# A graph layer with gathered neighbour rows: 74 instead of 64 rows fetched one by one, in three parts per block

## The chip, the cores and the metric

The kernel runs on one core of a Trainium2 chip. The metric is the device time of one execution in microseconds (us). Four runs of the kernel before gave 15966.83 to 15967.91 us, with a median of 15967.28 us. The profile is that of one execution, which took 15966.83 us; its span, from the first to the last instruction that the profile shows, is 15964.8 us.

## The reference: what is computed

There are N = 50,000 nodes with D = 128 features in float32, and E = 1,650,000 edges, sorted by destination (every node also has an edge to itself). Cut to what matters:

```python
Xs = X[src]                                   # one row of 128 floats per edge
m_data = Xs @ W_data.T + b_data
m_ctrl = Xs @ W_control.T + b_control
msg = jnp.where((edge_types == 0)[:, None], m_data, m_ctrl)
agg = jax.ops.segment_sum(msg, dst, num_segments=X.shape[0])
out = relu(agg + (X @ W_self.T + b_self))
x = _layernorm(x + out, axis=-1)
```

The kernel sums the raw rows of each node by edge type first and multiplies by the weights afterwards, so that its main work is to fetch one row of 512 bytes per edge and to add it to the right node.

## The kernel before, in words

The edges are cut into blocks. Block 0 and the last one ("plain" blocks) hold gathered edges alone; each of the 509 blocks between them holds 3,234 edges in Q = 2 steps, and a step has three kinds of edges:

- 12 chunks of 126 edges. POOL fetches a chunk with one indirect DMA (`gathers`, L473), so a block has 24 of them, in four passes of six. TensorE multiplies the rows by a one-hot matrix into `acc` (L492).
- F = 41 "fillers". An edge whose source is its own destination needs no gathered row, for the node's row is in `xT` anyway. `fill` (L306 to L336, VectorE) puts the 41 fillers into the slots of such edges, and `left_out_*` put the left-out rows back. The program branches at L934 to a slow general form (`general`) if some step holds fewer than F such edges.
- S = 64 single rows, one DMA of 512 bytes each, from a register address. They are issued by the queues of SP and ACT, 32 each per step. `offsets` (L433, VectorE) writes the 128 byte offsets of a block into the tile `at_x`, two blocks ahead and one more. `single_rows` (L435) loads 32 of them into registers of the engine with one TENSOR_LOAD (L442) and issues 32 row DMAs into the tile `yx` (L447), a register move and a DMA_DIRECT2D each. `yx` has four slots. TensorE waits for all of a block's single rows at L456 before their product L498.

The order of instructions on each engine is the order of the program text (`manual_schedule`). In the main loop (L607 to L655) the list of SP for block b is: load of `xT` for block b + 3 (L403, with the five block bases loaded into registers by L397 every fifth block, and seven loads of edge lists every tenth block); offsets and 32 rows of step 0 of block b + 2 (after pass 0); the store of the finished rows of block b - 1 (L556, after pass 2), which waits for VectorE's `o` (L555); offsets and 32 rows of step 1. The list of ACT is: offsets and 32 rows of step 0; the square root for block b - 1 (`root`, L547), which waits for VectorE's `mv`; offsets and 32 rows of step 1. VectorE's `store` (L553) waits for that square root, and after it VectorE makes `fill` for block b + 5, `offsets` for b + 3 and the sums of the next block.

The first offset load of a block waits for VectorE's `at_x`, and its first row DMA for TensorE's last use of the `yx` slot. POOL waits only for a free slot of its `y` tiles (10 slots of one pass each) and for its indices.

The four tiles `at_x` start at multiples of 16 bytes within their partition, as the built program places them (byte 177,856 and further in steps of 512), and so does `base_i` (byte 40,000), from which L397 loads the five bases of blocks b to b + 4, at byte 40,000 + 4b.

Of the kernel before, what the change touches and what calls it, by code (L numbers as in the profile page):

```python
# [2 lines left out]

# [10 lines left out]
U8 = mybir.dt.uint8  # L14
# [10 lines left out]
ROW = 4 * D  # L25
# [10 lines left out]
Q = 2  # L36
PASS = 6
B = 112
C = R * Q
F = 41  # L40
S = 64
X = Q * S
R1 = R + 1
C1 = Q * R1
SIZES = [126] * R
SIZE = sum(SIZES)
CE = Q * SIZE
BE = CE + Q * F + X
NBLK = 2 + (E - CE) // BE
# [7 lines left out]
AHEAD = 2  # L57
# [17 lines left out]
TBL = GROUPS * GB  # L75
# [3 lines left out]
def plain(b):  # L79

    return b == 0 or b >= NBLK - 1
# [6 lines left out]
def straight(ctx, tc, c, x, x_t, src_t, dst_t, etype_t, src_f, dst_f, etype_f, src_x, dst_first, first_p, out):  # L88
# [13 lines left out]
    nc = tc.nc  # L102
# [21 lines left out]
                   allow_small_or_imprecise_dtypes=True)  # L124
    FILL = Q * F + C1
    small = keep_ps.tile([P, 2 * W + F + 2 * FILL + 2], F32, name="small")
    num_ps, rank_no_ps = small[:, :2 * W], small[:, 2 * W:2 * W + F]
    lists = [small[:, 2 * W + F + i * FILL:][:, :FILL] for i in range(2)]
    sums_at = [small[:Q * F, 2 * W + F + 2 * FILL + i:][:, :1] for i in range(2)]

# [80 lines left out]
    def clear_sums():  # L211
        for t in sums:
            nc.vector.memset(t, 0.0)
            nc.vector.memset(t[0:3, 2, :], 1.0)
            nc.vector.memset(t[0:2, 2, :], 0.0)
# [80 lines left out]
    def spread_out(g):  # L296
        vd_g[g] = dram.tile([GS * F], F32, name="vd")
        nc.sync.dma_start(vd_g[g].rearrange("(s f) -> s f", f=F), vp_g.pop(g))

    def spread_in(g):  # L300

        v = eds.tile([P, GB, Q, F], F32, name="vf_all")
        nc.sync.dma_start(v.rearrange("p b q f -> p (b q f)"), row_bcast(vd_g.pop(g)))
        v_g[g] = v
# [33 lines left out]
    def left_out_columns(b):  # L338

        if not plain(b):  # L340
            pc = sums_at[b % 2]
            nc.tensor.matmul(pc, bys.pop(b).rearrange("p q f -> p (q f)"), ones_b[:, 0:1], start=True, stop=True)  # L342
            pcs[b] = pc

    def left_out_matrix(b):
        if not plain(b):
            z = fil.tile([Q * F, 2, P], BF16, name="z", bufs=RAHEAD + 1)
            at = fil.tile([Q * F, 1], F32, name="at")
            nc.vector.tensor_copy(at, pcs.pop(b))
            nc.vector.tensor_scalar(z.rearrange("p t n -> p (t n)"), node_no, at, None, op0=ALU.is_equal)  # L350
            zs[b] = z
# [25 lines left out]
    def steps_of(b):  # L377
        return [q for q in range(Q) if len(chunks_of(b, q))]
# [8 lines left out]

    idxs = {0: idx0}
    bys, pcs, zs, pls, bases, ats, ys = {}, {}, {}, {}, {}, {}, {}
    ohs, cnts, accs, xTs, pos, hs, mvs, sds = {}, {}, {}, {}, {}, {}, {}, {}  # L390

    BASES = 5

    def window(b):
        if b % BASES == 0:
            n = min(BASES, NBLK - b)
            _, regs = nc.values_load_multi_w_load_instructions(  # L397
                base_i[0:1, b:b + n], engines=[SP], min_val=0, max_val=N - B,
                skip_runtime_bounds_check_because="it was clamped to this")
            bases.update({b + i: at for i, at in enumerate(regs)})  # L400
        at = bases[b]
        xT = stp.tile([P, B], F32, name="xT", bufs=5)
        nc.sync.dma_start(xT, x_t[:, bass.ds(at, B)])  # L403
        xTs[b] = xT

    def onehot(b):
        g, i = divmod(b, GB)
        oh = ohp.tile([P, C1, 2 * W], F32, name="oh")
        nc.vector.tensor_tensor(oh, col_g[g][:, i, :, None].to_broadcast([P, C1, 2 * W]),  # L409
                                num_ps[:, None, :].to_broadcast([P, C1, 2 * W]), op=ALU.is_equal)  # L410
        ohs[b] = oh

    def counts(b):

        cnt = ohp.tile([P, Q, 2 * W], BF16, name="cnt")
        with nc.allow_low_precision(reason="whole numbers up to R1"):
            nc.vector.tensor_reduce(cnt, ohs[b].rearrange("p (q r) w -> p q w r", r=R1), AX.X, ALU.add)  # L417
        cnts[b] = cnt
# [1 line left out]


    ROW_SLOTS = AHEAD + 2
    TURN = S // 2
    RANGE = dict(min_val=0, max_val=(N - 1) * ROW, skip_runtime_bounds_check_because="where a node's row is")
    x_bytes = x.rearrange("n d -> (n d)").bitcast(U8)[None, :]
    fetched = [[tc.alloc_semaphore(f"fetched{j}_{i}") for i in range(ROW_SLOTS)] for j in range(2)]
# [5 lines left out]
            ats[b] = stp.tile([1, X], I32, name="at_x", bufs=AHEAD + 2)  # L432
            nc.vector.tensor_scalar(ats[b], one_g[g][:, i * X:(i + 1) * X], float(ROW), None, op0=ALU.mult)  # L433

    def single_rows(b, q):  # L435

        if q == 0:
            ys[b] = stp.tile([S, Q, D], F32, name="yx", bufs=ROW_SLOTS)
        both = []
        for j, (eng, dma) in enumerate(((SP, nc.sync), (ACT, nc.scalar))):  # L440
            at = j * TURN
            _, rows = nc.values_load_multi_w_load_instructions(  # L442
                ats[b][0:1, q * S + at:q * S + at + TURN], engines=[eng], **RANGE)
            both.append([(dma, fetched[j][b % ROW_SLOTS], at + k, row) for k, row in enumerate(rows)])
        for pair in zip(*both):
            for dma, sem, k, row in pair:
                copy = dma.dma_start(ys[b][k:k + 1, q, :].bitcast(U8), x_bytes[:, bass.ds(row, ROW)])  # L447
                copy.then_inc(sem, 16)
                tc.no_tile_sem_insts.add(copy.ins.name)
                tc.add_to_no_dep_group(f"single{b}", copy.ins)  # L450

    def rows_fetched(b):

        times = len(range(b % ROW_SLOTS or ROW_SLOTS, b + 1, ROW_SLOTS))
        for j in range(2):
            wait = nc.tensor.wait_ge(fetched[j][b % ROW_SLOTS], 16 * Q * TURN * times)  # L456
        tc.declare_fence(wait.ins, group=f"single{b}")


# [24 lines left out]
    def products(b, q, ks):  # L484
# [9 lines left out]
        if ks[-1] == of_step[-1]:  # L494
            if not plain(b):
                if q == 0:
                    rows_fetched(b)
                nc.tensor.matmul(acc[:, :2, :].rearrange("p t w -> p (t w)"), ys[b][:, q, :],  # L498
                                 ohs[b][:S, q * R1 + R, :], start=False, stop=True)
            for t in range(2):  # L500
# [49 lines left out]
    def store(b):  # L550
        mv = mvs.pop(b)
        rstd = stp.tile([B, 1], F32, name="rstd")
        nc.vector.reciprocal(rstd, sds.pop(b))  # L553
        o = stp.tile([B, D], F32, name="o")
        nc.vector.tensor_scalar(o, hs.pop(b), mv[:, 0:1], rstd, op0=ALU.subtract, op1=ALU.mult)  # L555
        nc.sync.dma_start(out[bass.ds(bases.pop(b), B), :], o)  # L556

    def find_bad():

# [36 lines left out]
    for b in range(1, RAHEAD):  # L596
        fill(b)
        left_out_columns(b)
        left_out_matrix(b)
        if b < AHEAD:  # L600
            onehot(b)
            counts(b)
            for q in range(Q):
                single_rows(b, q)
        if b == 1:
            clear_sums()
    for b in range(NBLK + 1):  # L607
        if b == NBLK - 1:
            find_bad()
        if b + 3 < NBLK:  # L610
            window(b + 3)
        g, i = divmod(b, GB)
        if i == 0 and g + 1 < GROUPS:
            load_edges(g + 1)
        if i == 3 and g + 1 < GROUPS:
            spread_out(g + 1)
        if i == 4 and g + 1 < GROUPS:
            spread_in(g + 1)
        if b > 0:
            add(b - 1, steps_of(b - 1)[-1])  # L620
        if b < NBLK:
            begin_sums(b)
        last = steps_of(b)[-1:]
        for q, (step, ks) in enumerate(passes_of(b)):
            if ks:
                products(b, step, ks)
            if q == 0 and b > 0:
                layer(b - 1)
            if q == 1:
                left_out_numbers(b + 1)  # L630
            if q == 3:
                left_out_columns(b + RAHEAD)
            if ks and step not in last and ks[-1] == chunks_of(b, step)[-1]:
                add(b, step)
            if q == 0 and b > 0:
                moments(b - 1)
            if q == 0 and b + AHEAD < NBLK:
                onehot(b + AHEAD)
            if q == 1 and b > 0:
                root(b - 1)  # L640
            if q == 2 and b > 0:
                store(b - 1)
            if q == 1 and b + AHEAD < NBLK:
                counts(b + AHEAD)
            if q == 2 and i == 2 and g + 1 < GROUPS:
                columns(g + 1)
            if q == 2:
                left_out_rows(b + 1)
                if b + RAHEAD < NBLK:
                    fill(b + RAHEAD)  # L650
            if q == 3:
                left_out_matrix(b + RAHEAD)
                offsets(b + AHEAD + 1)
            if q % 2 == 0 and not plain(b + AHEAD):
                single_rows(b + AHEAD, q // 2)  # L655


def general(ctx, tc, c, x, src, dst, etype, out):
# [331 lines left out]
```

## Time and profile before

| what | value |
|---|---|
| median of four runs | 15967.28 us |
| the profiled execution / its span | 15966.83 us / 15964.8 us |
| POOL busy | 12208.2 us (76%), 12,247 gathers (12,240 and 7) |
| VectorE (DVE) busy | 10893.8 us (68%) |
| TensorE (PE) busy | 8286.1 us (52%), granted clock 0.54 |
| ACT busy | 153.8 us (1%) |
| row DMAs by the queue of ACT / of SP | 32,576 / 32,576, 0.5 KB each |
| mean share of the 16 DMA engines | about 0.2 |

The profile lists an engine's busy time for its computing instructions only. Register loads, register moves and the issue of a DMA are done by the engine's own instruction queue (ACTq, SPq in the views) and are not counted as busy, so the 1% of ACT says nothing about how full its queue is. In the groups of instructions, a row gives the line, engine and operation, the count, the busy time, the mean of one, and the idle time ahead of them with its releaser. The view of one source line gives, for each engine, least, median and largest duration in ns and the first and last start.

### The profile page before, as it was taken

The numbers are of one execution on the slowest core, as the hardware profiler recorded it, in microseconds if no ns is written. First come the engines' busy times: TensorE is split into PE (matmuls) and PEld (weight loads), VectorE is DVE, ScalarE is ACT, GpSimd is POOL, SyncE is SP. The second block draws the span as 40 slices with busy tenths as digits, with TensorE's granted clock in tenths as the row PEclk, the third lists the DMA queues.
The fourth block names the chain that finished last, engine by engine and source line by source line (L and its number), as shares of the span: only waits on it lengthen the run. The fifth ranks groups of instructions, "written<-read, shape, count | busy, mean of one in ns | idle before, by whom it ended". The sixth has DMA issues, their size and how long they took to land.

```text
span 15964.8 us, 246443 instructions
## 1 busy us (share of the span) xinstructions
PE 8286.1 (52%) x35890; PEld 7100.4 (44%) x35891; DVE 10893.8 (68%) x14042; ACT 153.8 (1%) x517; POOL 12208.2 (76%) x12257
## 2 busy tenths in 40 slices
PE   3555555555555555555555555555555555555555
PEld 3444444444444444444444444444444444444444
DVE  8766666666666667666766666666666667666765
ACT  0000000000000000000000000000000000000000
POOL 7777777777777777777777777777777777777777
PEclk7555555555555555555555555555555555555555
DMA  2222222222222222222222222222222222222222
GB/s 62 60 59 60 59 60 59 60 60 59 59 60 59 59 60 59 60 59 60 59 59 59 59 60 58 60 60 59 59 60 59 59 60 58 60 59 60 59 59 56
DMA packets 895864, 944.21 MB, mean 59 GB/s; under 512 B 401739, under 2 KB 715928, under 8 KB 894220
## 3 DMA queue, kind: packets, MB, share of 16 engines
q0 software_dynamic: 587872, 791.74, 18.5%
q1 hardware_dynamic: 240758, 119.60, 2.9%
q10 hardware_dynamic: 65590, 17.01, 0.5%
q14 instruction: 1352, 11.08, 0.2%
q8 instruction: 292, 4.78, 0.1%
HBM read 896.86 MB, written 29.47 MB: 58 GB/s over the span
## 4 chain that ended last, share of the span: by engine, by line
POOL 59%; issue 19%; PE 10%; DMA 6%; DVE 4%; PEld 0%; ACTq 0%; POOLq 0%; PEldq 0%; ACT 0%; SPq 0%; DVEq 0%
POOL y L473 59%; PE acc L492 6%; DMA y<-in_x,idx 6%; PE po L531 2%; PE po L529 1%; DVE cnt L417 1%; PE po L528 1%; DVE h L537 0%; DVE h L538 0%; DVE st L540 0%; PE po L527 0%; DVE by L335 0%; ACTq L447 0%; PEld acc L492 0%; DVE m L316 0%
## 5 line engine op out<-in xcount | busy, mean ns | idle before, releaser
L473 POOL DMA_INDIRECT y<-in_x,idx x12240 | 12199.7, 997 | 3736.0 <-issue 3619.7
L492 PE MATMUL acc<-oh,y 126*128 126x120 f32 x24494 | 5873.8, 429 | 7031.1 <-PEq L480 7001.9
L492 PEld LDWEIGHTS acc<-oh,y 126*128 126x128 f32 x24494 | 5310.2, 326 | 7464.8 <-PEq L480 7424.6
L417 DVE TENSOR_REDUCE cnt<-oh 128x240 bf16<-128x3120 f32 x511 | 2959.0, 5791 | 0.1
L537 DVE COPY h<-po 112x128 f32<-112x128 f32 x511 | 149.0, 292 | 3334.9 <-PE po L531 3323.0
L409 DVE TENSOR_TENSOR oh<-col,small 128x3120 f32<-128x3120 f32 x511 | 1722.9, 3372 | 0.0
L508 DVE TENSOR_TENSOR sums<-acc,sums 128x180 f32 x1021 | 352.6, 345 | 1143.8 <-PE acc L501 1098.6
L335 DVE TENSOR_REDUCE by<-old 128x82 bf16<-128x1066 f32 x509 | 1073.5, 2109 | 17.6
L498 PE MATMUL acc<-oh,yx 64*128 64x120 f32 x2036 | 782.5, 486 | 0.0
L316 DVE TENSOR_TENSOR m<-rk,small 128x1066 f32<-128x1066 f32 x509 | 644.4, 1266 | 17.4
L319 DVE TENSOR_TENSOR new<-m,small 128x1066 f32<-128x1066 f32 x509 | 644.4, 1266 | 17.3
L323 DVE TENSOR_REDUCE v_new<-new 128x26 f32<-128x1066 f32 x509 | 642.9, 1263 | 17.3
L332 DVE TENSOR_TENSOR old<-m,small 128x1066 f32<-128x1066 f32 x509 | 640.2, 1258 | 0.0
L498 PEld LDWEIGHTS acc<-oh,yx 64*128 64x128 f32 x2036 | 500.4, 305 | 211.4 <-issue 207.3
L531 PE MATMUL po<-wmsgT,sums 128*112 128x128 f32 x2044 | 527.3, 403 | 0.0
L531 PEld LDWEIGHTS po<-wmsgT,sums 128*112 128x112 f32 x2044 | 383.1, 258 | 111.3 <-issue 94.7
L342 PE MATMUL small<-ones_b,by 128*82 128x1 bf16 x509 | 113.0, 222 | 609.6 <-DVE by L335 605.1
L342 PEld LDWEIGHTS <-by 128*82 128x82 bf16 x509 | 75.6, 149 | 659.5 <-DVE by L335 655.7
L529 PE MATMUL po<-bias,sums 3*112 3x128 f32 x1022 | 356.6, 445 | 1.5 <-DVE sums L508 1.5
L528 PE MATMUL po<-wselfT,xT 128*112 128x128 f32 x1022 | 317.6, 413 | 0.0
L521 DVE TENSOR_TENSOR sums<-pl,sums 128x336 f32<-128x336 f32 x509 | 258.3, 507 | 85.5 <-DVE sums L508 84.9
L547 ACT ACTIVATE sd<-mv,eps 112x1 f32<-112x1 f32 x511 | 150.6, 295 | 15690.9 <-DVE oh L409 7651.5
(119 smaller groups left out, 4201.9 us busy)
## 6 DMA issues: line engine op xcount, KB each, us to landing
yx<-in_x ACTq DMA_DIRECT2D x32576, 0.5 KB
yx<-in_x SPq DMA_DIRECT2D x32576, 0.5 KB
y<-in_x,idx POOLq DMA_INDIRECT x12240
xT<-in_x_t SPq DMA_DIRECT2D x511, 56.0 KB
out<-o SPq DMA_DIRECT2D x511, 56.0 KB
vf_all<-vd SPq DMA_DIRECT2D x52, 410.0 KB
s<-in_src_t SPq DMA_DIRECT2D x52, 130.0 KB
d<-in_dst_t SPq DMA_DIRECT2D x52, 130.0 KB
```

Of the source, the lines that this page charges most:

```text
L316: nc.vector.tensor_tensor(m, rk_g[g][:, i, :, None].to_broadcast([P, C1, F]), rank_no_ps[:, None, :].to_broadcast([P, C1, F]), op=ALU.is_e ...
L319: nc.vector.tensor_tensor(new.rearrange("p (q r) f -> p q r f", r=R1), m.rearrange("p (q r) f -> p q r f", r=R1), vf.rearrange("p (q f) -> ...
L323: nc.vector.tensor_reduce(v, new, AX.X, ALU.add)
L332: nc.vector.tensor_tensor(old, m, cb[:, :, None].to_broadcast([P, C1, F]), op=ALU.mult)
L335: nc.vector.tensor_reduce(by, old.rearrange("p (q r) f -> p q f r", r=R1), AX.X, ALU.add)
L409: nc.vector.tensor_tensor(oh, col_g[g][:, i, :, None].to_broadcast([P, C1, 2 * W]), num_ps[:, None, :].to_broadcast([P, C1, 2 * W]), op=AL ...
L417: nc.vector.tensor_reduce(cnt, ohs[b].rearrange("p (q r) w -> p q w r", r=R1), AX.X, ALU.add)
L473: copy = nc.gpsimd.indirect_dma_start(out=y[:r, k % PASS, :].bitcast(U8), out_offset=None, in_=x_rows, in_offset=bass.IndirectOffsetOnAxis ...
L492: nc.tensor.matmul(acc[:, :2, :].rearrange("p t w -> p (t w)"), y[:r, k % PASS, :], ohs[b][:r, column(k), :], start=k == of_step[0], stop= ...
L498: nc.tensor.matmul(acc[:, :2, :].rearrange("p t w -> p (t w)"), ys[b][:, q, :], ohs[b][:S, q * R1 + R, :], start=False, stop=True)
L529: nc.tensor.matmul(po, a[0:3, 2, :B], bias, start=False, stop=False)
L531: nc.tensor.matmul(po, a[:, t, :B], c["wmsgT"][:, t * D:(t + 1) * D], start=False, stop=t == 1)
```

## The change

S becomes 74: of each step's single rows SP fetches 36 and ACT 38. F becomes 42. A block then holds 3,256 edges, there are 505 full blocks instead of 509 (507 with the plain ones, instead of 511), and the last block holds 2,696 edges in 22 chunks instead of 870 in 7.

A block's single rows are no longer loaded by step but by engine: in the list of offsets stand first the 72 of SP, then the 76 of ACT, and each engine takes its own in three parts (24, 24 and 24 for SP; 25, 25 and 26 for ACT), after passes 0, 1 and 2. ACT's offsets start at elements 72, 97 and 122 of `at_x`. The tile has 148 elements of 4 bytes, and its slots again start at multiples of 16 bytes. The store of the finished rows stands after pass 3 now, behind all of SP's rows. The order of the other work is the same. In the changed file L442, L447, L547, L553 and L556 are L446, L451, L551, L557 and L563.

```diff
-F = 41
-S = 64
+F = 42
+TURNS = (36, 38)
+S = sum(TURNS)
+LOADS = 3
...
-    def single_rows(b, q):
-
-        if q == 0:
+    def single_rows(b, part):
+
+        if part == 0:
             ys[b] = stp.tile([S, Q, D], F32, name="yx", bufs=ROW_SLOTS)
         both = []
         for j, (eng, dma) in enumerate(((SP, nc.sync), (ACT, nc.scalar))):
-            at = j * TURN
-            _, rows = nc.values_load_multi_w_load_instructions(
-                ats[b][0:1, q * S + at:q * S + at + TURN], engines=[eng], **RANGE)
-            both.append([(dma, fetched[j][b % ROW_SLOTS], at + k, row) for k, row in enumerate(rows)])
-        for pair in zip(*both):
-            for dma, sem, k, row in pair:
-                copy = dma.dma_start(ys[b][k:k + 1, q, :].bitcast(U8), x_bytes[:, bass.ds(row, ROW)])
+            n = Q * TURNS[j]
+            k0, k1 = part * n // LOADS, (part + 1) * n // LOADS
+            at = Q * sum(TURNS[:j])
+            _, rows = nc.values_load_multi_w_load_instructions(ats[b][0:1, at + k0:at + k1], engines=[eng], **RANGE)
+            both.append([(dma, fetched[j][b % ROW_SLOTS], *divmod(k0 + k, TURNS[j]), sum(TURNS[:j]), row)
+                         for k, row in enumerate(rows)])
+        for pair in zip_longest(*both):
+            for dma, sem, q, k, at, row in filter(None, pair):
+                copy = dma.dma_start(ys[b][at + k:at + k + 1, q, :].bitcast(U8), x_bytes[:, bass.ds(row, ROW)])
                 copy.then_inc(sem, 16)
...
-            wait = nc.tensor.wait_ge(fetched[j][b % ROW_SLOTS], 16 * Q * TURN * times)
+            wait = nc.tensor.wait_ge(fetched[j][b % ROW_SLOTS], 16 * Q * TURNS[j] * times)
...
-        nc.sync.dma_start(out[bass.ds(bases.pop(b), B), :], o)
+        os_[b] = o
+
+    def store_rows(b):
+        nc.sync.dma_start(out[bass.ds(bases.pop(b), B), :], os_.pop(b))
...
-            for q in range(Q):
-                single_rows(b, q)
+            for part in range(LOADS):
+                single_rows(b, part)
...
-            if q % 2 == 0 and not plain(b + AHEAD):
-                single_rows(b + AHEAD, q // 2)
+            if q < LOADS and not plain(b + AHEAD):
+                single_rows(b + AHEAD, q)
+            if q == LOADS and b > 0:
+                store_rows(b - 1)
...
-        ones[1:] = steps[:, :, SIZE + F:].reshape(TBL - 1, X)
+        single = steps[:, :, SIZE + F:]
+        ones[1:] = np.concatenate([single[:, :, sum(TURNS[:j]):][:, :, :n].reshape(TBL - 1, Q * n)
+                                   for j, n in enumerate(TURNS)], axis=1)
```

More of the change, by code (lines that the diff above doesn't have):

```diff
@@ L2 @@
 from contextlib import ExitStack
+from itertools import zip_longest
 import concourse.bacc as bacc
@@ L389, in straight @@
     bys, pcs, zs, pls, bases, ats, ys = {}, {}, {}, {}, {}, {}, {}
-    ohs, cnts, accs, xTs, pos, hs, mvs, sds = {}, {}, {}, {}, {}, {}, {}, {}
+    ohs, cnts, accs, xTs, pos, hs, mvs, sds, os_ = {}, {}, {}, {}, {}, {}, {}, {}, {}
     BASES = 5
@@ L422, in straight @@
     ROW_SLOTS = AHEAD + 2
-    TURN = S // 2
     RANGE = dict(min_val=0, max_val=(N - 1) * ROW, skip_runtime_bounds_check_because="where a node's row is")
```

## The prediction

> **What bounds the kernel now.** I read the chain that ended last first, then the two costliest groups.
>
> ```profile
> POOL 59%; issue 19%; PE 10%; DMA 6%; DVE 4%; PEld 0%; ACTq 0%; POOLq 0%; PEldq 0%; ACT 0%; SPq 0%; DVEq 0%
> ...
> L473 POOL DMA_INDIRECT y<-in_x,idx x12240 | 12199.7, 997 | 3736.0 <-issue 3619.7
> L492 PE MATMUL acc<-oh,y 126*128 126x120 f32 x24494 | 5873.8, 429 | 7031.1 <-PEq L480 7001.9
> ```
>
> POOL's gathers lead the chain. One takes 997 ns, and the idle time ahead of them is nearly all "issue": POOL waits for nobody, it needs 0.30 us between two gathers. The view of line L473 has the first gather at 3.2 us and the first of the last seven at 15938.1: 15,934.9 us for 12,240, **1.302 us each, 31.25 us per block of 24**. The PE row says the reverse: PE waits for rows. So POOL is saturated, and any engine that needs under 31.25 us per block is free.
>
> Next come the queues, which the busy shares leave out. The timeline of one block (from the start of a line's first row DMA; rows of one line are merged), for ACT and then for SP:
>
> ```profile
> 8013.16 10.67 ACTq L447 DMA_DIRECT2D yx<-in_x  x32
> 8023.93 0.30 ACT L547 ACTIVATE sd<-mv,eps 112x1 f32<-112x1 f32 x1 [28.90 <-DVE oh L409]
> ```
>
> ```profile
> 8014.04 0.36 SPq L403 DMA_DIRECT2D xT<-in_x_t  x1
> 8016.62 10.66 SPq L447 DMA_DIRECT2D yx<-in_x  x32
> 8032.94 0.34 SPq L556 DMA_DIRECT2D out<-o  x1
> ```
>
> 32 rows take some 10.7 us, and 2 us pass ahead of them. That is the load of their offsets, in the view of line L442, whose three durations are least, median and largest in ns:
>
> ```profile
> L442 ACTq TENSOR_LOAD <-at_x x1018: 2112/2145/2417, 16.9 to 15862.6; - x170
> L442 SPq TENSOR_LOAD <-at_x x1018: 1864/2066/2272, 26.9 to 15872.9; - x170
> ```
>
> All those loads start at a multiple of 16 bytes. The changed ones don't, so I looked for loads that don't now. L397 loads five bases at byte 40,000 + 4b. Here are those for b = 20, 25, 30 and 35, and the last, of a single one, for b = 510; modulo 16 their bytes are 0, 4, 8, 12 and 8.
>
> ```profile
> L397 SPq TENSOR_LOAD <-base_i x1: 789/789/789, 555.7 to 555.7; - x1
> L397 SPq TENSOR_LOAD <-base_i x1: 1342/1342/1342, 706.0 to 706.0; - x1
> L397 SPq TENSOR_LOAD <-base_i x1: 1345/1345/1345, 860.5 to 860.5; - x1
> L397 SPq TENSOR_LOAD <-base_i x1: 1330/1330/1330, 1016.9 to 1016.9; - x1
> L397 SPq TENSOR_LOAD <-base_i x1: 537/537/537, 15854.6 to 15854.6; - x1
> ```
>
> **This decides my forecast.** In the whole trace each of the 26 loads of five at a multiple of 16 takes 0.75 to 0.96 us, and each of the 76 others 1.33 to 1.55, with the same registers in turn; so it is the address. Misaligned, one register takes 0.54 and five 1.34: **0.20 us per further register**. Aligned, five take 0.79 and 32 take 2.07: 1.28 us for 27 more, **0.19 us per further group of four** (0.047 per register). I read it as accesses of 0.2 us, which bring four registers from an aligned start and one otherwise. At offset 12, one register and then an aligned four would be two accesses, as at offset 0, but the row shows 1.33 and not 0.79: the load doesn't fall back into fours on its way.
>
> A page of the Trainium skill speaks against every load here: "Runtime: NRT & Kernel Launch", section "Instruction fetch mechanics", puts register loads at about 200 ns per register, even in bulk. The 2.07 us for 32 contradict it for aligned loads (it would give 6.4), and 0.20 per further register agrees for misaligned ones. By the rule for all three loads (76 x 0.2 = 15.2 us) ACT would need 41.2 us per block and the kernel some 20,900 us, an estimate.
>
> **The change part by part.**
>
> *Fewer gathers.* Edges: (1,650,000 - 3,024) / 3,256 gives 505 full blocks and 2,696 edges over. Gathers: 24 x 506 + 22 = 12,166, against 12,247. 81 x 1.302 = 105.5 us less on POOL, all on the path as long as POOL sets it.
>
> *ACT's list.* Three loads. The first starts at byte 288 of its tile (a multiple of 16): 25 registers, 2.145 - 7 x 0.047 = 1.81 us. The second starts at byte 388, the third at 488: 4 and 8 modulo 16. 25 misaligned registers: 1.34 + 20 x 0.20 = 5.34, and ACT's loads take 1.04 times SP's (2.145 / 2.066): 5.55 us. 26: 5.76 us. Together 13.1 us, against 4.3 now.
> Rows: within a part, from the third row on, ACT issues one per 0.3245 us (mean in the trace; median 0.318), and 0.41 us per part lies around its load and first row (a part of 32 takes 12.95 us in the mean: 2.15 + 32 x 0.3245 + 0.41). 76 rows: 24.7 + 3 x 0.41 + 0.1 for the square root's start = 26.0 us. **ACT needs 26.0 + 13.1 = 39.1 us per block**, against 25.9 now (with over 5 us of waiting), and POOL 31.25. Nothing hides the difference: ACT becomes the bound.
>
> *SP's list.* 72 rows at 0.3275 us = 23.6; 0.16 around each of three loads = 0.5; three loads of 24 (bytes 0, 96, 192, all aligned): 3 x (2.066 - 8 x 0.047) = 5.1; the store 0.55 and `xT` 0.6 with what lies around them; the bases 0.25, edge lists and spreads 0.4 in the mean. 31.0 us: just below POOL and well below ACT. The store now stands behind all rows. At its old place SP waited for `o` (1601.0 us in the waits of SP's queue), with 32 rows queued behind it. `o` comes 22 us after the block's `at_x`, and SP's rows now take about 29: the wait goes, and what it held up, `xT` for three blocks ahead, is not needed for long. Price nothing, between -0.1 and +0.3 us per block.
>
> *VectorE and PE.* 42 instead of 41 fillers lengthen five operations of 7.2 us together (L316, L319, L323, L332, L335) by 2.4%: 0.17 us. VectorE is busy 21.3 of 31.25 us, so this is hidden; without cover it is 88 us. PE's single-row product has 74 rows for 64 and the same 120 columns; the rows of L492 (126) and L498 (64) show no growth with rows. Nothing.
>
> *Where the wait shows.* The square root stands between ACT's first and second part, and VectorE's `store` waits for it, with fill, the next `at_x` and the sums queued behind it. From there to the next `mv` VectorE needs 20 us, and to the next `at_x` 10 us; ACT brings 39 and 28 us of its own work in that time. So ACT never waits: VectorE waits for ACT, PE for VectorE, and POOL for slots.
>
> **Sum.** The first square root starts at 116.7 us; ACT then has 503 blocks of rows: 503 x 39.1 = 19,667. About 60 us follow the last row (two blocks' products, sums and stores; now it is 89 us, with gathers at POOL's pace in it). Span 19,840 or, with a third of a block already issued at 116.7, 19,828, and 2.0 us around the span as now: **19,830 us, 24% more than before**. The profiled execution lies 0.45 us below the median, so no correction.
> Bounds: with rows at the median 0.318, no factor 1.04 and 0.18 per register (five misaligned against five aligned are three accesses more for 0.55 us), the loads take 12.0 us and ACT 37.5: 19,030. With 0.24 per register (ACT's 2.145 against 0.463 for its single load of `bad`, L934, are seven accesses more) and 0.33 per row, the loads take 14.4 us and ACT 40.8: 20,690.
>
> **The rivals.**
>
> *No fee for misalignment in long loads* (the other side). Against it: 76 of 76 rows of five. For it: no misaligned load of more than five is in the trace. Loads of 1.81, 1.81 and 1.86 make ACT 31.5 us, a hair over POOL. The point that decides is 31.25: at 0.3 us less, which the median row pitch would give, POOL stays the bound and all of the gain comes, 15,966.8 - 105.5 = **15,861 us** (-0.7%). At 31.5, 503 x 31.5 + 177 = 16,020. Chance 0.07, of which 0.05 faster and 0.02 within 0.2%, about what a measurement of this kernel can tell from no change.
>
> *A fixed fee per misaligned load*: 1.34 - 0.79 = 0.55 us, twice per block. ACT 26.0 + 1.81 + 2.36 + 2.41 = 32.6 us: 503 x 32.6 + 177 = **16,570 us**. Against it: a single misaligned register pays 0.07 (0.54 against 0.47 for SP's load of `bad`). Chance 0.07.
>
> *Two accesses per misaligned four*, since it lies in two 16-byte lines: 6 x 0.19 more per load, ACT 33.9 us, **17,230 us**. Against it: five would then take 0.98. Chance 0.05.
> The Trainium skill's "SBUF — State Buffer", section "Specifications (TRN2)", has 16-byte lines and a penalty for each new line, which would favour this case; it states no figure for register loads.
>
> *The general form starts*, so that the change doesn't do what it says. It needs a step with fewer than 42 self-edges among its 1,512 gathered ones; counted in the inputs, the smallest has 43. Chance nil.
>
> **How the numbers follow.** Per-register loads: 0.80, at 19,830 us. No fee: 0.07. Fixed fee: 0.07. Two accesses: 0.05. 0.01 for anything else. The likeliest case alone leaves out no more than 2 in 10, so the range is its own: 19,030 to 20,690 us. Faster 0.05, same 0.02, slower 0.93.
>
> **What would show it.** In the view of L446, ACT's loads: one third near 1.8 us, two thirds at 5.3 to 5.9, while SP's stay near 1.7. In the waits, VectorE's reciprocal L557 for ACT's square root: thousands of us, where the trace now has 6.4. POOL's idle time ahead of L477 no longer all "issue", about 8 us per block. If ACT's misaligned loads take 2 us, I am wrong at the first step, and the time is near 16,000. If they are long but the time is not, ACT's row issue must be shorter than now.

## The result, and the profile after

The changed kernel takes 19875.35 us (median of 8 runs, 19871.03 to 19878.22) against 15967.64 us (11 runs) of the kernel before beside it: a ratio of 1.2447, 95% interval 1.2434 to 1.246. The forecast was 19,830, with 19,030 to 20,690. The profiled execution took 19877.22 us, its span is 19875.5.

The page of the changed kernel, first the chain that ended last (by engine), then three of its groups:

```profile
ACTq 85%; issue 13%; ACT 1%; DVE 1%; PE 0%; DMA 0%; SPq 0%; DVEq 0%
...
L477 POOL DMA_INDIRECT y<-in_x,idx x12144 | 12094.0, 996 | 7697.7 <-PE acc L496 3791.0
L496 PE MATMUL acc<-oh,y 126*128 126x120 f32 x24332 | 4215.1, 344 | 0.1
...
L557 DVE RECIPROCAL rstd<-sd 112x1 f32<-112x1 f32 x507 | 83.0, 164 | 6890.2 <-ACT sd L551 6890.2
```

The chain has moved from POOL to ACT's instruction queue, which the engine's busy share of 1% doesn't show. POOL's idle time ahead of its gathers has doubled, to 15.2 us per block. Some 7 us of it are the 0.30 us between gathers, as before, and 8 us are waits, most of them for PE to give a slot back; PE waits for VectorE, and VectorE's reciprocal for ACT's square root. Each gather takes what it took.

The view of the changed line L446, over the whole execution and, in the last line, for one block of ACT (8000 to 8042 us), where least, median and largest are the three loads of that block:

```profile
L446 ACTq TENSOR_LOAD <-at_x x1515: 1887/5593/6113, 16.9 to 19833.3; - x190
L446 SPq TENSOR_LOAD <-at_x x1515: 1419/1677/1913, 27.4 to 19800.9; - x190
```

```profile
L446 ACTq TENSOR_LOAD <-at_x x3: 2002/5577/5822, 8003.7 to 8032.2; - x3
```

On the same engine, in the same block, 25 registers take 2.00 us from a multiple of 16 bytes and 5.58 us from four bytes past one. By position in the block the medians are 2.00, 5.59 and 5.85 us, together 13.44. The timeline of ACT shows the block's length, from one square root to the next (in brackets the idle time of the computing part ahead of it):

```profile
8003.67 0.29 ACT L551 ACTIVATE sd<-mv,eps 112x1 f32<-112x1 f32 x1 [39.16 <-issue]
8009.38 33.33 ACTq L451 DMA_DIRECT2D yx<-in_x  x76
8042.81 0.30 ACT L551 ACTIVATE sd<-mv,eps 112x1 f32<-112x1 f32 x1 [38.85 <-issue]
```

Over all blocks it is 39.23 us in the mean. 13.44 of them are loads, 25.8 rows and what lies around them.

### The profile page after: what moved, and what is told of

Read it like the earlier page. It is cut to its first block, busy times and chain, and to the rows that moved or that the text cites. A ratio compares the mean times of both kernels' runs of the same rounds, so it can differ in the third digit from the quotient of the medians.

```text
span 19875.5 us, 265771 instructions
## 1 busy us (share of the span) xinstructions
PE 5765.3 (29%) x35633; PEld 5425.4 (27%) x35634; DVE 10831.7 (54%) x13919; ACT 152.6 (1%) x513; POOL 12117.3 (61%) x12176
## 4 chain that ended last, share of the span: by engine, by line
ACTq 85%; issue 13%; ACT 1%; DVE 1%; PE 0%; DMA 0%; SPq 0%; DVEq 0%
ACTq L451 52%; ACTq L446 33%; ACT sd L551 1%; DVE cnt L420 0%; PE acc L496 0%; DVE by L338 0%; ACTq L551 0%; DVE m L319 0%; DVE new L322 0%; DVE v_new L326 0%; DVE old L335 0%; DVE oh L412 0%; PE po L535 0%; DMA first_i<-in_dst_first 0%; PE po L533 0%
## 5 line engine op out<-in xcount | busy, mean ns | idle before, releaser
L496 PE MATMUL acc<-oh,y 126*128 126x120 f32 x24332 | 4215.1, 344 | 0.1
L496 PEld LDWEIGHTS acc<-oh,y 126*128 126x128 f32 x24332 | 3967.9, 255 | 0.3 <-PE po L588 0.2
L345 PE MATMUL small<-ones_b,by 128*84 128x1 bf16 x505 | 116.1, 230 | 12904.1 <-DVE by L338 12904.1
L557 DVE RECIPROCAL rstd<-sd 112x1 f32<-112x1 f32 x507 | 83.0, 164 | 6890.2 <-ACT sd L551 6890.2
L338 DVE TENSOR_REDUCE by<-old 128x84 bf16<-128x1092 f32 x505 | 1071.3, 2121 | 17.5
L319 DVE TENSOR_TENSOR m<-rk,small 128x1092 f32<-128x1092 f32 x505 | 652.4, 1292 | 17.2
L322 DVE TENSOR_TENSOR new<-m,small 128x1092 f32<-128x1092 f32 x505 | 652.3, 1292 | 17.2
L326 DVE TENSOR_REDUCE v_new<-new 128x26 f32<-128x1092 f32 x505 | 651.9, 1291 | 17.2
L335 DVE TENSOR_TENSOR old<-m,small 128x1092 f32<-128x1092 f32 x505 | 648.2, 1283 | 0.0
L502 PE MATMUL acc<-oh,yx 74*128 74x120 f32 x2020 | 462.7, 317 | 0.0
L502 PEld LDWEIGHTS acc<-oh,yx 74*128 74x128 f32 x2020 | 386.1, 237 | 0.0
```

The lines of the kernel that those rows point to most:

```text
L319: nc.vector.tensor_tensor(m, rk_g[g][:, i, :, None].to_broadcast([P, C1, F]), rank_no_ps[:, None, :].to_broadcast([P, C1, F]), op=ALU.is_e ...
L322: nc.vector.tensor_tensor(new.rearrange("p (q r) f -> p q r f", r=R1), m.rearrange("p (q r) f -> p q r f", r=R1), vf.rearrange("p (q f) -> ...
L326: nc.vector.tensor_reduce(v, new, AX.X, ALU.add)
L338: nc.vector.tensor_reduce(by, old.rearrange("p (q r) f -> p q f r", r=R1), AX.X, ALU.add)
```

## The experiments

**Theory (address)**: a register load that starts at a multiple of 16 bytes brings four registers per access of some 0.2 us, any other load one; with its two misaligned loads ACT's list takes 39 us per block, 8 us more than POOL's 31.25. **Rivals**: ACT can't hold three loads and 76 rows, whatever the address (size); a misaligned load takes single registers up to the next multiple of 16 and fours from there.

One thing has to be known ahead of the times. On the chips that the experiments got, the kernel before took 23,247 us (e1 to e4), 23,316 (e1_again, e4_again), 23,364 (e6, e7, c1) and 22,921 (e10 to e12), not 15,967. So times are compared within such a set, or by their ratio to the kernel before of the set, and their absolute size only in the last one.

**e1_aligned, e1_again: all loads at multiples of 16.**

```diff
+PARTS = ((0, 24, 48, 72), (0, 24, 48, 76))
...
-            k0, k1 = part * n // LOADS, (part + 1) * n // LOADS
+            k0, k1 = PARTS[j][part:part + 2]
```

> The changed kernel, but ACT takes its 76 offsets in parts of 24, 24 and 28, so that every register load starts at a multiple of 16 bytes; nothing else differs. Theory (address): ACT's loads fall to 1.7 to 2.0 us each, 5.6 us together, ACT needs 25.8 + 5.6 = 31.4 us per block against POOL's 31.25, and the time is 15,860 to 16,000 us. Rival (size: three parts and 76 rows are too much for ACT, whatever the address): loads of 5.6 us and 19,875 us as in the changed kernel. Rival (half of it: a misaligned load costs a fixed fee): the trace after has excluded it.

> The same kernel as e1_aligned (ACT in parts of 24, 24 and 28, all loads at multiples of 16 bytes), once more, since its first runs were on a chip on which the kernel before took 23,247 us. Theory (address): where the kernel before takes 15,967 us, ACT's loads take 1.7 to 2.0 us, its list 25.8 + 5.6 = 31.4 us per block, and the time is 15,860 to 16,000 us. Rival (size): 19,875 us.

Measured: 24908.89 us, ratio 1.0717 (1.0699 to 1.0735), and again 25031.1 us, 1.073 (1.0712 to 1.0748). The loads are as the address has them, but neither theory's time came. The chain of e1 that ended last, by engine, and the views of its lines L447 (loads) and L452 (rows), least, median and largest in ns:

```profile
SPq 58%; issue 36%; DMA 2%; PE 2%; DVE 1%; ACTq 0%; PEldq 0%; another core or an unknown queue 0%; ACT 0%; DVEq 0%
```

```profile
L447 ACTq TENSOR_LOAD <-at_x x1515: 3/1702/2270, 17.0 to 24801.8; - x190
```

```profile
L452 ACTq MOVE yx<-in_x x38380: 2/29/1460, 18.7 to 24812.0; - x200
...
L452 SPq DMA_DIRECT2D yx<-in_x x36360: 1/228/1740, 29.4 to 24882.5; - x200
```

A register move, 29 to 38 ns on ACT in the profile of before, lasts up to 1460 ns here, and others 2 ns. Of ACT's 38,380 moves 3,550 last over 0.2 us, 3,159 of them 0.65 to 0.76 us: on this chip the two queues stand still again and again, in steps of 0.7 us. In the stretches of 4 us in which three gathers start, ACT issues 1.26 rows per us in the mean, and 2.28 in those with none; in the profile of before it is 2.06 with three gathers. The kernel before is slower on this chip too, and in e1 it is SP's queue and not ACT's that leads the chain. So these times say little of ACT's list.

**c1_after: the changed kernel on such a chip.**

> The changed kernel once more, beside the kernel before at 23,247 and 23,316 us on the chips of the experiments, as the partner of e1 and e3. Theory (address): ACT's misaligned loads take 5.6 and 5.85 us here too, and the time lies near that of e3 (27,394 us), well above e1's 24,909. Rival (the chips' own slowness hides the loads): within 1% of e1.

Measured: 25711.06 us, ratio 1.1015 (1.0959 to 1.107), with ACT's loads at a median of 5.54 us. By these ratios (e1: 1.0717, on another chip) aligned loads are worth some 3%. Neither time that was expected came: the stalls cover most of what the long loads cost, as I read it, and with ACT's loads aligned SP's queue sets the pace.

**e2_before_shifted: the kernel before, misaligned.**

```diff
-            ats[b] = stp.tile([1, X], I32, name="at_x", bufs=AHEAD + 2)
+            at = stp.tile([1, X + 4], I32, name="at_x", bufs=AHEAD + 2)
+            ats[b] = at[:, 3:3 + X]
```

> The kernel before, but the list of offsets starts three elements into its tile, so that every register load of 32 starts at 12 modulo 16; nothing else differs. Theory (address, one access per register for the whole load): a load takes 0.54 + 31 x 0.20 = 6.8 us instead of 2.1 on SP and 7.0 on ACT; SP's list goes from 27.2 to 36.6 us per block and ACT's from 25.9 to 35.5, so SP sets the pace: 509 x 36.6 + 150 = 18,780 us. Rival (the load takes one register and goes on in fours from the next multiple of 16): 2.3 us per load, SP 27.6 us, hidden behind POOL, no change at 15,967 us. Rival (size): no change either, since the sizes are those of before.

Measured: 25315.92 us, ratio 1.0894 (1.0876 to 1.0912). The view of its line L443:

```profile
L443 ACTq TENSOR_LOAD <-at_x x1018: 4847/6994/7393, 16.4 to 25167.8; - x170
L443 SPq TENSOR_LOAD <-at_x x1018: 4870/6644/6915, 27.0 to 25240.8; - x170
```

The same 32 registers, moved by 12 bytes: 6.99 us instead of 2.15 on ACT (expected 7.0), 6.64 instead of 2.07 on SP (6.8). Going on in fours after one single register would give 2.3 us. Both rivals fall here: the sizes are those of before. The time can't be read beyond its sign.

**e3_swapped: 38 rows per step by SP, 36 by ACT.**

```diff
-TURNS = (36, 38)
+TURNS = (38, 36)
```

> The changed kernel with the shares swapped: SP fetches 38 rows per step and ACT 36. SP's second and third load then start at bytes 100 and 200 of the tile (misaligned), and all of ACT's (bytes 304, 400, 496) at multiples of 16. Theory (address): SP's loads take 1.8, 5.4 and 5.6 us and its list 24.9 + 0.5 + 12.8 + 1.8 = 40.0 us per block, ACT's loads 1.75 us each; 503 x 40.0 + 150 = 20,270 us. Rival (ACT's queue can't hold 38 rows per step): ACT is relieved of 4 rows and the time falls to 16,100 us or less.

Measured: 27394.22 us, ratio 1.1795 (1.1775 to 1.1815); now SP has the long loads. The view of L446:

```profile
L446 ACTq TENSOR_LOAD <-at_x x1515: 3/1670/1951, 16.9 to 27259.3; - x190
L446 SPq TENSOR_LOAD <-at_x x1515: 709/4911/5737, 27.7 to 27344.4; - x190
```

The long loads went with the addresses from ACT to SP, and relieving ACT didn't help: on the same chip e1 took 24908.89 us. SP fetches the 38 rows here, so that the number of rows isn't tested by this run; e11 does that.

**e4_aligned73, e4_again: 36 + 37 rows per step, all aligned.**

```diff
-TURNS = (36, 38)
+TURNS = (36, 37)
...
+PARTS = ((0, 24, 48, 72), (0, 24, 48, 74))
...
-            ats[b] = stp.tile([1, X], I32, name="at_x", bufs=AHEAD + 2)
+            at = stp.tile([1, X + 2], I32, name="at_x", bufs=AHEAD + 2)
+            ats[b] = at[:, :X]
...
-            k0, k1 = part * n // LOADS, (part + 1) * n // LOADS
+            k0, k1 = PARTS[j][part:part + 2]
```

> 73 single rows per step, 36 by SP and 37 by ACT, ACT in parts of 24, 24 and 26, all loads at multiples of 16 bytes; 42 fillers; 12,172 gathers instead of 12,247. Theory (address; queues that need less than 31.25 us per block cost nothing): ACT's list 24.0 + 1.3 + 5.5 = 30.8 us, SP's 30.8 us, POOL sets the pace with all of its gain: 15,967.3 - 75 x 1.302 = 15,870 us. Rival (size): near 19,600 us. Rival (the queues are too near to POOL's pace and their jitter costs): 15,900 to 16,000 us.

> The same kernel as e4_aligned73 (36 + 37 single rows per step, all loads aligned), once more for the same reason. Theory (address): ACT's and SP's lists take 30.8 us each, POOL sets the pace with all of its gain: 15,870 us, faster than both kernels. Rival (size): near 19,600 us. Rival (queues so near to POOL's pace that their jitter costs): 15,900 to 16,000 us.

Measured: 24759.98 us, 1.0649 (1.0632 to 1.0667), and 24891.31 us, 1.0672 (1.0654 to 1.069). On these chips it is slower than before, not faster. That a version with aligned loads beats the kernel before is therefore not shown anywhere.

**e6 and e7: fewer instructions.** Two kernels that differ in ACT's parts alone, with SP's rows as one DMA and a sixth of the chunk products, to see whether the number of instructions makes the stalls. Against the changed kernel (e6) and e1 (e7):

```diff
+            if j == 0:
+                if part == 0:
+                    copy = dma.dma_start(ys[b][0:0 + TURNS[j]], x[:Q * TURNS[j], :].rearrange("(p q) d -> p q d", q=Q))
...
+                continue
...
+            if k not in (of_step[0], of_step[-1]):
+                continue
             r = REST_ROWS[k] if b == NBLK - 1 else SIZES[k % R]
             nc.tensor.matmul(acc[:, :2, :].rearrange("p t w -> p (t w)"), y[:r, k % PASS, :], ohs[b][:r, column(k), :],
```

> The changed kernel with work left out so that fewer instructions are recorded: SP fetches its 72 rows of a block as one plain DMA of fixed rows, and TensorE multiplies only the first and last of a step's 12 gathered chunks (all are gathered). ACT's list is that of the changed kernel: parts of 25, 25 and 26, the second and third load misaligned. It is to be compared with e7, which differs in the parts alone. Theory (address): ACT needs 39.2 us per block as in the changed kernel, 503 x 39.2 + 145 = 19,860 us, on this chip too. Rival (on these chips a limit on recorded instructions, 10.6 per us, sets every time): 154,000 instructions then take 14,500 us, so it can't be seen and the time is again ACT's or POOL's. Rival (these chips issue rows or gathers slower in themselves): above 21,000 us.

> As e6, with ACT's parts 24, 24 and 28, so that all its loads start at multiples of 16 bytes. Theory (address): loads of 1.7 to 2.0 us, ACT 31.4 us per block beside POOL's 31.25, 15,860 to 16,000 us. Rival (size: three parts and 76 rows are too many for ACT whatever the address): 19,860 us as e6. Rival (these chips are slower in themselves): above 18,000 us.

Measured: 25936.15 us and 23775.73 us. With 150,988 instructions instead of 265,771 e6 is no faster than the changed kernel on the same chip (c1, 25711.06 us): the idea of a limit on recorded instructions is wrong. Aligned loads are worth 2,160 us here, but the stalls are still there, and the expected times didn't come.

**e10, e11, e12: few gathers.** What was left in e7 beside ACT's list were the gathers. e10 is e6, e11 is e7 and e12 is e4, each gathering and multiplying only the first and last chunk of a step.

```diff
-        y = gathers(b, ks)
         of_step = chunks_of(b, q)
+        ks = [k for k in ks if k in (of_step[0], of_step[-1])]
+        y = gathers(b, ks)
```

> As e6 (SP fetches 72 fixed rows per block as one DMA, two chunks per step multiplied), and POOL gathers only those two chunks of each step, 4 per block instead of 24, since on these chips the queues' rows stall while gathers run. ACT's list is that of the changed kernel: 25, 25 and 26 rows, second and third load misaligned. POOL needs 5.2 us per block, so ACT's list sets the pace if anything of it is right. Theory (address): loads of 2.0, 5.6 and 5.85 us, 39.2 us per block, 503 x 39.2 + 130 = 19,850 us. Rival (the chips are slower in themselves, gathers or not): above 21,000 us.

> As e10, with ACT's parts 24, 24 and 28, all aligned; the addresses are the only difference. Theory (address): loads of 1.75, 1.75 and 1.95 us, 31.3 us per block, 503 x 31.3 + 130 = 15,870 us. Rival (size: three loads of 24 to 28 registers and 76 rows): within 1% of e10. Rival (a fixed fee of 0.55 us per misaligned load): 1.1 us per block, 550 us less than e10.

> e4 (36 + 37 single rows per step, all loads aligned, both queues fetching their rows, the store behind SP's rows) with 4 gathers per block and two products per step. It measures what the two lists need where POOL doesn't set the pace. Theory: SP 3 x 9.66 + 1.8 = 30.8 us per block, ACT 24.0 + 1.3 + 5.3 = 30.6; 504 x 30.8 + 130 = 15,650 us, which is under POOL's 31.25 us per block: with all gathers POOL would set the pace at 15,870 us. Rival (both queues together disturb each other): over 31.25 us per block, above 15,880 us.

Measured: **e10 19851.85 us** (19723.79 and 19979.90), **e11 15857.40 us** (15719.02 and 15995.79), **e12 15812.35 us** (15716.28 and 15908.42). The two runs of each kernel lie 1.2 to 1.8% apart, and those of the first two within 1% of the times expected, 19,850 and 15,870. In e10 and e11 no move of ACT lasts over 0.04 us, so the stalls are gone; in e12 they are gone on ACT, and 477 of SP's 36,432 moves last over 0.2 us. Loads of e10 (L453), e11 (L454) and e12 (L448), one fence each, over the whole execution:

```profile
L453 ACTq TENSOR_LOAD <-at_x x1515: 1893/5558/5952, 16.7 to 19683.2; - x190
```

```profile
L454 ACTq TENSOR_LOAD <-at_x x1515: 1654/1752/2062, 16.6 to 15681.7; - x190
```

```profile
L448 ACTq TENSOR_LOAD <-at_x x1518: 1647/1762/2419, 16.9 to 15652.7; - x190
L448 SPq TENSOR_LOAD <-at_x x1518: 1172/1676/1892, 27.1 to 15681.6; - x190
```

The three loads of one block, of e10 (25, 25 and 26 registers) and of e11 (24, 24 and 28):

```profile
L453 ACTq TENSOR_LOAD <-at_x x3: 1993/5529/5865, 8010.1 to 8034.5; - x3
```

```profile
L454 ACTq TENSOR_LOAD <-at_x x3: 1685/1740/1992, 8006.0 to 8025.7; - x3
```

By position, e10's three loads have medians of 2.00, 5.56 and 5.85 us, together 13.41; e11's 1.75, 1.69 and 2.00, together 5.44: 7.97 us less. From square root to square root the mean is 38.94 us in e10 and 30.98 in e11: 7.96 us less. **So the difference lies in the loads alone, and 503 x 7.96 = 4,004 us, against 4,005 between the two profiled executions (19723.79 and 15719.02).** Of the 7.97 us, 0.24 come from the first load, which is aligned in both and has a register less in e11, and 7.7 from the two that are moved to multiples of 16 bytes; of these two one is shorter by a register and the other longer by two. A fixed fee would have given 550 us. In the chain of e10 that ended last, ACT's queue has 78%:

```profile
ACTq 78%; issue 14%; DVE 6%; PE 1%; ACT 1%; DVEq 0%; DMA 0%; SPq 0%
ACTq L458 48%; ACTq L453 30%; DVE cnt L420 2%; ACT sd L561 1%; DVE by L338 1%; DVE m L319 0%; DVE new L322 0%; DVE v_new L326 0%; DVE old L335 0%; PE po L545 0%; PE po L543 0%; PE acc L506 0%; DVE stats L234 0%; DVE cb L280 0%; DVE stats L235 0%
```

e12 has both queues' full lists and takes 30.86 us per block (expected 30.8), under POOL's 31.25. Its profiled execution of 15716.28 us lies 0.4% above the 15,650 expected, which is less than its two runs differ.

## Why the prediction was right, point by point

*POOL is saturated, and an engine under 31.25 us per block is free.* Right for an engine above it: once ACT needed more, POOL's wait for slots rose by about the difference, 8 us per block. That an engine just below it costs nothing beside all the gathers is not shown by these runs.

*A misaligned load costs 0.20 us per register.* Right. 25 registers were put at 5.55 us and took 5.59, 26 at 5.76 and took 5.85. With e2, whose 32 take 6.99, seven more registers cost 1.40 us, 0.20 each. The five bases of L397 were enough to see it, since an address that cycles through all four remainders came with its own control. The Trainium skill's 200 ns per register ("Runtime: NRT & Kernel Launch", "Instruction fetch mechanics") agrees with misaligned loads (0.20 here) and not with aligned ones (24 registers in 1.69 us in e11). The page (section "The ~15µs preamble/postamble breakdown") speaks of register loads from HBM, while `at_x` is an on-chip tile.

*The first load, 1.81 us.* Mis-sized: 2.00. I took 0.047 us per register, but 25 is six fours and one over, and the one over costs as much as a four. The loads of e11 and e12 fit this: 24 registers take 1.69 us, 26 (six fours and two over) 2.22, and 28 (seven fours) only 2.00.

*Rows, 26.0 us.* 25.8. *After the last row, 60 us.* 28: it starts at 19847.4. Loads of +0.3 and rows of -0.2 leave 39.23 us per block against 39.1, which is 65 us over 503 blocks. The -32 us at the end take half of that back, and the third of a block (12 us) that was taken off was not there to take. So 19,875 against 19,830: that the time is met within 0.3% is in part luck, since the errors partly cancel; the two long loads, on which the forecast rests, were each met within 2%.

*Where the wait shows.* Right. VectorE's reciprocal waits for ACT's square root 6890 us in all, in the page above; in the waits of the kernel before it was

```profile
DVE rstd L553 <- ACT sd L547: 6.4, 8, 1.7
```

*SP's list, 31.0 us, and the moved store.* SP's part of 24 rows with its load takes about 9.6 us in the mean, which makes some 30.7 per block with the 1.8 us put for its other work. The wait for `o` went, as forecast; the waits of SP's queue (us in all, times, longest), first in the kernel before, then in the changed one:

```profile
SPq L556 <- DVE o L555: 1601.0, 397, 23.7
```

```profile
SPq L446 <- DVE sums L525: 4400.8, 495, 15.3
...
SPq L563 <- DVE o L559: 158.2, 312, 5.7
```

SP waits 158 us for `o` (1601.0 before), and 4401 us at its loads, because VectorE is late. The view names `sums` there; in the block near 8000 us that is shown above, `at_x` is done at 8020.99 us and SP's load starts at 8021.0, so it is `at_x` that SP waits for. The store's place has not been tried by itself.

*The rivals.* No fee, the fixed fee and two accesses per four are excluded by the loads' durations: they put 25 misaligned registers at 1.8, 2.4 and 3.0 us, and these took 5.59. What the other side needed, all loads aligned, has been built: ACT's list then takes 30.98 us (e11), and 30.86 us are enough for both queues with 73 rows (e12), both with 4 gathers per block. That POOL would then set the pace at 15,860 to 15,870 us on a chip like that of the result is worked out from this, not shown.

## What to carry to other kernels

Look at the byte address of every register load: a list that is cut into parts should have each part start at a multiple of 16 bytes and, if it can, hold a multiple of four values. An engine with 1% busy can be the bound, for register loads and DMA issues aren't counted: add up its queue by lines (loads, moves, issues) per block and compare it with the pace of the kernel. When the trace lacks the size that a change brings, look for a small operation whose address or length varies by itself; a hundred short loads gave the price of a misaligned one here within 2%.

## What the runs showed that I had not expected

The same kernel took 15,967 us on the chip of the result and 22,921 to 23,364 us on the others. There, the queues of SP and ACT stand still in steps of 0.7 us while gathers run: 24 gathers per block held ACT's list of 31 us at 47 us (e7), and 4 per block, on another of these chips, left it alone (e11). The gathers themselves are no slower there: in e1 they take 999 ns, and POOL starts them 1.30 us apart (median). Fewer recorded instructions didn't change it (e6, e7). What in the gathers does it, and why only on these chips, stays open.
